# Inverse roots of norms and chains: from Sqrt on ScalarE to a power on GpSimd

## The chip, the cores and the metric

The kernel runs on one core of one Trainium2 chip. The metric is the device time of one execution in microseconds; three runs of the kernel before gave 1999.21, 1999.24 and 1999.36, median 1999.24. A profile of one further execution (1999.32 us) is what all readings below come from. Its own span, from the first to the last instruction, is 1997.5 us.

## The reference, cut to what matters

Four layers act on `x` of shape (8, 512, 32, 32), so on 8 images of 512 channels and 1024 pixels. The second works like this for each image, and inverse square roots appear in its group norm:

```python
# layer 0: attention without softmax, scaled by the largest singular value
f_x = relu(batchnorm(conv1x1(x, Wf, bf), gamma_f, beta_f))   # rsqrt(var + 1e-5)
g_x = relu(batchnorm(conv1x1(x, Wg, bg), gamma_g, beta_g))   # rsqrt(var + 1e-5)
h_x = conv1x1(x, Wh, bh)
z = einsum('bcn,bcm->bnm', f_x, g_x)
attn = z / svd(z)[0]
x = conv1x1(einsum('bnm,bcm->bcn', attn, h_x), Wv, bv) + x
# layer 1: group norm, then attention with softmax over 1024 pixels
h = group_norm(x)                                            # rsqrt(var + 1e-5)
q, k, v = wq @ h, wk @ h, wv @ h
x = x + wp @ (softmax(q.T k / sqrt(512)) applied to v)
# layer 2: a second attention, 128 channels, batch norm with given statistics
# layer 3: sign(x) times sign(W), batch norm with given statistics, a PReLU
```

## The kernel before, in words

All weights stay in SBUF, and the work runs in two parts.

The early part (to about 213 us) loads the eight images, computes the projections `f`, `g` and `h` of layer 0 and their batch statistics, and builds the combined weights of layer 1 (`wu`, `wo`). The norm of `f` and `g` needs one inverse root on 128 x 2 numbers (name `r0`). The singular value of `z` is found per pair of images by a chain of squarings of 128 x 128 matrices (`chain`, four of them): each step is two products on TensorE, an eviction of them from PSUM by VectorE or ScalarE, and a trace that is stored in a column of `tr`. A chain takes the root of its first trace near its start and needs it only at its end, where Ln and Exp on ScalarE turn the traces into the scale `rsig`. The first chain runs in the early part; the three others are slipped in between the matmuls of the images.

The main part goes through the eight images in the order 6, 7, 0, 1, 2, 3, 4, 5 (`fast`). For one image it runs these stages:

- `scores1`: the first attention's scores, with Strassen-like products of seven terms (`seven`), the exponentials on ScalarE (L347, L510, L511), one addition of two blocks on GpSimd (L341), and the row sums `esum` on VectorE (L515, L516). Between these, `enter` adds layer 0's result to the next image, takes its statistics and computes its group norm, with one inverse root on 128 x 4 numbers (name `r1`). The scale and bias that come out are used first when the next image is normalized (L440, L442), in the middle of `values1`.
- `make_v`: products of `h` and `wo`, again of seven terms. The first term of each is copied out of PSUM by ScalarE (L331) before TensorE may add the next to the same bank. After the first of the terms, `inverse_sums` adds the row sums over the partitions with a matmul (L775) and inverts them (L783).
- `values1` (L536), then the second attention (`project2` at L621 and L633, `scores2` at L754 with exponentials at L761, `values2` at L874), and `close2` and `leave` for the last layer.

The order on each engine is set by a scheduler that goes by its own estimates of durations, but for TensorE in the early chain, where the order of the program is kept. [...]

The inverse root is a helper, `rsqrt_eps`: VectorE writes `v = var + eps`, ScalarE takes `Sqrt` (L219), VectorE inverts it, and four more operations of VectorE make one Newton step. It is used for `r3` and `r2` (given statistics, at 12 us), for `r0`, and for `r1` once for each image. Beside the main path, a fallback with general softmax runs only when a check of the row sums fails; it isn't run here.

[...] `Sqrt`, `Ln` and `Exp` are in different loaded sets in this program, and the build puts a table load ahead of each change of set (the rows ACT_TABLE_LOAD).

## Time and profile before

| | |
|---|---|
| time, median of 3 | 1999.24 us |
| span of the profiled execution | 1997.5 us |
| mean granted clock of TensorE | 0.988 of full speed |
| ScalarE table loads | 29, of 1.283 us each |
| of these under `rsqrt_eps` (L219) | 9 |
| under the chains' root (L971) | 2 |
| Sqrt instructions | 11 in `rsqrt_eps`, 4 in chains, about 0.20 us each |
| idle times of TensorE over 0.06 us | 44, 44.1 us in all |

A row of a timeline reads: start in us, length in us, engine, line, operation, the tile written and the tiles read, shape, and how many instructions in a row were merged; in brackets the idle time before it and the work that ended it. fp32 matmuls stand in the trace as two records each. A row of busy times by stretch reads: the stretch, its length, then busy microseconds and number of instructions of TensorE, its weight loads, VectorE, ScalarE and GpSimd, then the granted clock of TensorE, the share of the DMA engines and GB/s.

### The profile page before, as it was taken

How to read it: one execution, taken by the hardware profiler on the slowest of the kernel's cores; microseconds unless marked ns; L12 is line 12 of the kernel's file. 1: busy time of each engine (PE TensorE's matmuls, PEld its weight loads, DVE VectorE, ACT ScalarE, POOL GpSimd, SP SyncE). 2: the span in 40 equal slices, each digit the busy share in tenths (PEclk: the TensorE clock that was granted, in tenths of full speed). 3: DMA queues.
4: the chain of work that ended last, by engine and by line, in shares of the span. 5: the costliest groups of instructions: out<-in, count | busy, mean ns of one | idle time of the engine just before them, and what ended most of it. 6: DMA issues, size and time to landing. Idle time of an engine off the chain costs nothing.

```text
span 1997.5 us, 16654 instructions
## 1 busy us (share of the span) xinstructions
PE 1936.9 (97%) x6262; PEld 997.3 (50%) x6262; DVE 1111.1 (56%) x1822; ACT 536.6 (27%) x838; POOL 187.9 (9%) x152
## 2 busy tenths in 40 slices
PE   8999899999999999999999999999999999999997
PEld 2377346544465445454465446444545446544653
DVE  3245577437863487536752576337653675256626
ACT  2132222134220342123311432034212431134114
POOL 0000000200011000200011000200020001101110
PEclk9989999999999999999999999999999999999999
DMA  9320000002000020001100020002000110010001
GB/s 330 127 74 1 6 6 11 1 11 85 6 11 0 11 84 17 0 0 32 68 11 1 22 77 13 0 11 85 11 0 1 42 53 11 0 32 21 11 1 54
DMA packets 26711, 66.99 MB, mean 34 GB/s; under 512 B 3760, under 2 KB 4016, under 8 KB 25984
## 3 DMA queue, kind: packets, MB, share of 16 engines
q1 hardware_dynamic: 25968, 65.09, 9.5%
q8 instruction: 51, 0.84, 0.2%
q0 software_dynamic: 224, 0.33, 0.1%
q10 hardware_dynamic: 432, 0.43, 0.1%
q14 instruction: 36, 0.29, 0.0%
HBM read 38.51 MB, written 18.87 MB: 29 GB/s over the span
## 4 chain that ended last, share of the span: by engine, by line
PE 92%; DVE 4%; ACT 3%; issue 1%; DMA 0%; DVEq 0%; ACTq 0%
PE bank L369 37%; PE bank L536 19%; PE bank L874 6%; PE bank L621 6%; PE bank L754 6%; PE bank L1122 4%; PE bank L633 3%; PE bank L650 3%; PE bank L392 2%; PE bank L670 1%; PE bank L925 1%; PE wide L1178 1%; PE bank L1232 1%; PE bank L926 1%; PE bank L775 1%; DVE e L326 1%
## 5 line engine op out<-in xcount | busy, mean ns | idle before, releaser
L536 PE MATMUL bank<-e,vt 128*128 128x512 f32 x768 | 334.0, 593 | 0.0
L536 PEld LDWEIGHTS bank<-e,vt 128*128 128x128 f32 x768 | 145.0, 190 | 175.4 <-issue 171.7
L369 PE MATMUL bank<-ut,h 128*128 128x512 f32 x384 | 183.3, 598 | 4.7 <-ACT e L331 4.7
L369 PE MATMUL bank<-us,hs 128*128 128x512 f32 x256 | 121.3, 596 | 0.5 <-DVE us L298 0.5
L326 DVE TENSOR_TENSOR e<-bank,e 128x512 f32<-128x512 f32 x128 | 87.7, 685 | 61.2 <-PE bank L369 59.9
L874 PE MATMUL bank<-e,tpg 128*128 128x512 f32 x256 | 114.6, 595 | 0.0
L754 PE MATMUL bank<-tpg 128*128 128x512 f32 x256 | 114.6, 592 | 0.0
L369 PEld LDWEIGHTS bank<-ut,h 128*128 128x128 f32 x384 | 70.6, 190 | 87.7 <-issue 73.5
L621 PE MATMUL bank<-xt,tpg 128*128 128x512 f32 x256 | 113.6, 592 | 0.0
L369 PE MATMUL bank<-wo,h 128*128 128x256 f32 x384 | 95.7, 389 | 18.3 <-ACT vt L331 18.3
L761 ACT ACTIVATE e<-bank 128x512 f32<-128x512 f32 x128 | 76.4, 597 | 88.3 <-PE bank L754 88.3
L369 PE MATMUL bank<-h,wu 128*128 128x512 f32 x192 | 92.1, 603 | 3.4 <-DVE h L442 3.4
L326 DVE TENSOR_TENSOR vt<-bank,vt 128x512 f32<-128x512 f32 x64 | 44.0, 687 | 90.2 <-PE bank L369 89.3
L341 POOL TENSOR_TENSOR ut<-ut 128x512 f32<-128x512 f32 x16 | 21.7, 1359 | 734.1 <-ACT ut L322 734.1
L766 DVE TENSOR_TENSOR esum<-esum,e 128x1024 f32<-128x1024 f32 x48 | 58.8, 1226 | 54.8 <-ACT e L761 54.8
L369 PEld LDWEIGHTS bank<-wo,h 128*128 128x128 f32 x384 | 72.4, 193 | 31.1 <-ACT vt L331 21.5
L341 POOL TENSOR_TENSOR e<-e 128x512 f32<-128x512 f32 x32 | 41.6, 1301 | 441.1 <-ACT e L320 388.3
L874 PEld LDWEIGHTS bank<-e,tpg 128*128 128x128 f32 x256 | 48.0, 190 | 63.9 <-issue 63.9
L754 PEld LDWEIGHTS bank<-tpg 128*128 128x128 f32 x256 | 48.6, 190 | 60.8 <-issue 58.6
L621 PEld LDWEIGHTS bank<-xt,tpg 128*128 128x128 f32 x256 | 47.9, 190 | 56.4 <-issue 55.0
L369 PEld LDWEIGHTS bank<-us,hs 128*128 128x128 f32 x256 | 47.3, 190 | 57.5 <-issue 51.4
L660 ACT ACTIVATE sg<-xt,rb 128x512 f16<-128x512 f32 x64 | 43.8, 717 | 103.6 <-DVE xt L652 100.9
(306 smaller groups left out, 2996.4 us busy)
## 6 DMA issues: line engine op xcount, KB each, us to landing
xt<-in_x SPq DMA_DIRECT2D x56, 512.0 KB
out<-both SPq DMA_DIRECT2D x64, 256.0 KB
rfull<-rsum SPq DMA_DIRECT2D x64, 128.0 KB
f_dram<-f SPq DMA_DIRECT2D x8, 256.0 KB
fb<-f_dram SPq DMA_DIRECT2D x8, 256.0 KB
w<-in_w SPq DMA_DIRECT2D x1, 1024.0 KB
q<-in_w_q SPq DMA_DIRECT2D x1, 1024.0 KB
k<-in_w_k SPq DMA_DIRECT2D x1, 1024.0 KB
```

The source lines that it names most:

```text
L326: nc.vector.tensor_tensor(dst, ps, u, ALU.add)
L341: nc.gpsimd.tensor_tensor(c22, c22, c12, ALU.add)
L369: mm(out=ps[:, q * w : (q + 1) * w], lhsT=lt(ka, kb, q, k), rhs=rhs(ka, kb, q, k), start=first and q == 0 and k == 0, stop=last and k == 1 ...
L536: mm(out=ps, lhsT=a[:, t, bass.ts(r_, P)], rhs=e[t], start=first and t == 0, stop=last and t == NTH - 1, skip_group_check=True,)
L621: mm(out=ps, lhsT=sbw["tpg"][:, cc, bass.ts(i, P)], rhs=xt[:, cc, half(h)], start=cc == 0, stop=cc == CC - 1,)
L633: mm(out=ps[:, i, :], lhsT=xt[:, cc, bass.ts(4 * h + i, P)], rhs=sbw["tpg"][:, cc, 2 * P : 3 * P], start=cc == 0, stop=cc == CC - 1,)
L650: mm(out=ps, lhsT=sbw["z"][:, bass.ts(oc, P)], rhs=att, start=True, stop=True)
L754: mm(out=ps, lhsT=pt[:, 0, bass.ts(t, P)], rhs=tt[:, 0, half(h)], start=True, stop=True,)
L761: nc.scalar.activation(e[:, half(h)], ps, AF.Exp, scale=float(P) ** -0.5)
L766: nc.vector.tensor_tensor(esum, esum, e, ALU.add)
L874: mm(out=banks[h], lhsT=gt[:, t, :], rhs=es[t][:, half(h)], start=t == 0, stop=t == NT - 1,)
L1122: mm(out=banks[i][side(h), :], lhsT=w0[i][:, cc, :], rhs=xt[:, cc, half(h)], start=cc == 0, stop=cc == CC - 1,)
```

## The change

The Sqrt on ScalarE and the reciprocal on VectorE after it are replaced, in both places, by one instruction of GpSimd that raises the number to the power -0.5. The exponent is a constant tile, set once by a memset. The Newton step of the norms stays as it was. The chain's Newton step for the root becomes one for the inverse root: four operations of VectorE where there were a reciprocal, three others and another reciprocal. Nothing else is edited; the scheduler places the instructions anew.

```diff
+    minus_half = const.tile([P, CC], F32, tag="minus_half", name="minus_half")
+    nc.gpsimd.memset(minus_half, -0.5)
...
         nc.vector.tensor_scalar(v, var, EPS, None, ALU.add)
-        nc.scalar.activation(e, v, AF.Sqrt)
-        nc.vector.reciprocal(r, e)
+        nc.gpsimd.tensor_tensor(r, v, minus_half[:, 0:n], ALU.pow)
         nc.vector.tensor_tensor(e, r, r, ALU.mult)
         nc.vector.tensor_tensor(e, e, v, ALU.mult)
         nc.vector.tensor_scalar(e, e, -0.5, 1.5, ALU.mult, ALU.add)
...
         root, half_ = column("root"), column("half_")
-        nc.scalar.activation(root, tr[:, 0:1], AF.Sqrt)
-        nc.vector.reciprocal(half_, root)
+        nc.gpsimd.tensor_tensor(root, tr[:, 0:1], minus_half[:, 0:1], ALU.pow)
+        nc.vector.tensor_tensor(half_, root, root, ALU.mult)
         nc.vector.tensor_tensor(half_, half_, tr[:, 0:1], ALU.mult)
-        nc.vector.tensor_tensor(root, root, half_, ALU.add)
-        nc.vector.tensor_scalar(root, root, 0.5, None, ALU.mult)
-        nc.vector.reciprocal(root, root)
+        nc.vector.tensor_scalar(half_, half_, -0.5, 1.5, ALU.mult, ALU.add)
+        nc.vector.tensor_tensor(root, root, half_, ALU.mult)
```

Line numbers in the text are those of the kernel before. In the kernel after, lines from about 202 on stand two further down as far as the helper, one further down from there to the chain's root, and the same after it.

## The prediction

> **What bounds the kernel now.** I read the page's busy times first, then the idle times ahead of TensorE, and then, for each idle time, the timelines of ScalarE and VectorE over the same microseconds.

> ```profile
> PE 1936.9 (97%) x6262; PEld 997.3 (50%) x6262; DVE 1111.1 (56%) x1822; ACT 536.6 (27%) x838; POOL 187.9 (9%) x152
> ...
> L219 ACT ACT_TABLE_LOAD x9 | 11.5, 1283 | 2.3 <-issue 2.2
> ```

> TensorE sets the time; ScalarE is busy 27%, so taking work off it is worth only what TensorE waits for it. The groups of ScalarE by shape show 29 table loads in all (9 at L219, 6 at L761, 4 at L998, 4 at L1001, 3 at L510, 2 at L971, 1 at L347), 37.2 us at 1283 ns. Where does TensorE wait behind one? Its timeline has 44 idle times, 44.1 us together. Seven lie at one place, the start of `make_v`, where the copy at L331 must empty a PSUM bank before TensorE may add to it. First ScalarE, then TensorE, of the second image:

> ```profile
> 536.94 1.06 ACT L511 ACTIVATE e<-e 128x1024 f32<-128x1024 f32 x1
> 538.02 1.28 ACT L219 ACT_TABLE_LOAD   x1
> 539.32 0.20 ACT L219 ACTIVATE r_e<-r_v 128x4 f32<-128x4 f32 x1
> 539.54 1.28 ACT L510 ACT_TABLE_LOAD   x1
> 540.84 0.63 ACT L510 ACTIVATE e<-e 128x512 f32<-128x512 f32 x1
> 541.37 0.57 ACT L331 COPY vt<-bank 128x512 f32<-128x512 f32 x1
> ```
> ```profile
> 536.42 1.89 PE L369 MATMUL bank<-wo,h 128*128 128x256 f32 x8
> 541.99 2.07 PE L369 MATMUL bank<-wo,h 128*128 128x256 f32 x4 [3.68 <-ACT vt L331]
> 544.03 1.74 PE L775 MATMUL bank<-esum,ones 128*64 128x512 f32 x4
> 545.71 1.99 PE L369 MATMUL bank<-so,hs 128*128 128x256 f32 x8
> 547.54 0.38 PE L925 MATMUL bank<-cur 128*128 128x128 f32 x2
> ```

> The Sqrt and the return to Exp stand between two exponentials, so the copy comes 2.8 us late. The next image's norm does not need its result for another 15 us or more. The last image has no next norm; it is the control:

> ```profile
> 1847.32 1.89 PE L369 MATMUL bank<-wo,h 128*128 128x256 f32 x8
> 1849.88 1.99 PE L369 MATMUL bank<-wo,h 128*128 128x256 f32 x8 [0.68 <-ACT vt L331]
> 1851.81 1.08 PE L775 MATMUL bank<-esum,ones 128*64 128x512 f32 x4
> 1852.81 1.99 PE L369 MATMUL bank<-so,hs 128*128 128x256 f32 x8
> 1854.64 1.67 PE L369 MATMUL bank<-wo,h 128*128 128x256 f32 x7
> ```

> The wait is 0.68 there, and the same 4 records of L775 take 1.0 instead of 1.7. So the idle time costs twice: the granted clock, by stretches, falls after it (the number ahead of the last two columns).

> ```profile
> 538.60:542.00 3.40, 0.01 (x1) 0.01 (x1) 2.46 (x11) 3.30 (x5) 0.00 (x0) 1.00 0.00 0
> 542.10:545.40 3.30, 3.30 (x8) 1.36 (x8) 3.14 (x4) 0.00 (x0) 0.00 (x0) 0.50 0.00 0
> ...
> 777.60:784.30 6.70, 6.04 (x14) 3.16 (x13) 5.82 (x4) 0.00 (x0) 0.00 (x0) 0.50 0.00 0
> 995.00:1000.00 5.00, 3.36 (x15) 1.69 (x14) 4.69 (x9) 2.29 (x4) 0.00 (x0) 1.00 0.00 0
> ```

> [...] L511 ends at 538.00, the load starts at 538.02, and the Sqrt starts 0.02 after the load. [...] 0.50 in stretches of 3.4 to 6.8 us after the three waits of 3.68, and 1.00 after the four of 1.64. [...]

> **The change part by part.**

> *Table loads.* In the order in which the changed kernel's instructions stand, ScalarE has 9 loads where it had 29: one at the start, and L998 and L1001 for each of four chains. Twenty are gone, 25.7 us of ScalarE. The six at L761 are worth nothing on the path: from the first matmul of L621 to the first of L874 it is 50.2 us in the third image, which has no such load (853.31 to 903.52), and 50.2 in the fourth, which has (1069.44 to 1119.65). L347 and L971 have no TensorE wait of L331's kind behind them. So what counts is `make_v`.

> I price it over the same 28 records: 16 of `wo,h` (in images one to seven 4 of them come later, 0.87 us), 4 of L775, 8 of `so,hs`. Last image: 1847.32 to 1854.64, 7.32. Second: 536.42 to 547.54 plus 0.87, 11.99. The first and third, read the same way, 298.47 to 310.75 and 771.21 to 784.30, give 13.15 and 13.96. The fourth to seventh give 8.38 (993.76 to 1001.27 plus 0.87). The excess over the control is 5.83, 4.67 and 6.64, sum 17.1, and 4 x 1.06 = 4.2.

> How much of it goes? In the first three images L510 would start at 538.00, the copy end near 539.15, and TensorE start then, 0.84 after it stopped. It then has all 8 records (1.73) and would reach L775 at 540.9. But L775 needs the row sums, and the new order on VectorE puts three L557 subtractions between them: from 537.4, small operations of 0.1, three of 0.62 and two sums of 1.2 give 542.1. A wait of 1.25 stays, with 0.15 above the control at the copy: 1.4 an image, 4.3 in three. Gain 17.1 - 4.3 = 12.8. It takes for granted that pieces of 0.84 and 1.25 no longer bring the half clock, as 1.64 and 1.81 (at 486.6) bring none. In the four others the sums end at 998.2 and TensorE reaches L775 at 998.14: all 4.2 goes. Together 17.0.

> *The power on Pool* (call p the time from VectorE's `r_v` to its reading of the result). The trace has none. From below: the nearest small Pool rows are 0.10 us (a memset of one column) and 0.31 (the 128x128 select), so p is at least about 0.3. [...] I take [...] p = 0.8[...].

> What p delays: in the new order VectorE reads the result one operation (0.62) after `r_v`, so past p = 0.5 VectorE stands still with the row sums queued behind it. At 0.8 that is 0.3 in each of three images, and 0.1 in each of four, where TensorE has as much slack: 1.3 in all. The first-layer norm (101 us) and the first image's norm (207 us) are on the path: Sqrt and reciprocal took 0.44 from the end of `r_v` (101.10 to 101.54), the power 0.8: 0.4 each, 0.8. In the first chain the power's reader is now ahead of the eviction at L945 (114.58); at p = 0.8 that ends near 115.7, and its product starts at 115.81: nothing. The other three roots land where VectorE has about 1 us idle (367) or more; even behind one Pool sum (1.27) they delay no matmul. [...]

> *The rest.* One VectorE operation fewer (0.15 to 0.18) per norm and root, hidden or in the 0.44; one memset of 0.1 at 5 us on an idle Pool. On Pool the power stands between the `e` sums and the `vt` sums, which start 15 us later (552.58 in the second image). No DMA is added; on SP one `fb` load moves one place.

> Sum: 17.0 - 1.3 - 0.8 = 14.9 of the span of 1997.5. The three timed runs are 1.7 to 1.9 us above that span, and I carry the difference over: 1999.24 - 14.9 = 1984.3, so 1984.

> **The rivals.**

> *Slower: the power is slow.* Place: VectorE's in-order queue after each `r_v`. Every microsecond of p costs about 10: three images, four images, two norms on the path and the first chain. The gain is 2.9 at p = 2.0 (12.8 - 4.5, 4.2 - 5.2, -3.2, -1.2), so it decides from p = 2.3. At p = 5 it is 1999.2 + 27 = 2026, and the half clock would return on top. For it: nothing in the trace bounds p closely. Against it: the Pool's simple rows run at 1.27 us for 512 columns, so its fixed cost is small.

> *A new wait keeps the clock low.* The wait for the row sums takes over, [...] the first three images keep the half clock. Then a stall of 4.85 (541.99 and 544.03 against 4 records' 0.87) shrinks to 2.4: 3 x 2.45 + 4.2 - 2.1 = 9.4, that is 1990. A middling p of 1.5 gives 7.9, or 1991, in the same region.

> *The loads were hidden anyway*, or waiting moves with them: 1999. Against it stands the control.

> **How the numbers follow.** Fast power with the clock kept, 0.60: 1984, by itself 1979 to 1988 (all 21.3 of excess gone at best; p to 1.1). New wait or middling p, 0.20: 1988 to 1995. Hidden or cancelling, 0.05: within 4 us of before. Slow power, 0.15. The measurement tells about 0.2%, 4 us, from no change. So faster 0.80, same 0.05, slower 0.15. The range takes in the first two cases and p to 2: 1979 to 1997, which leaves out the slow power and a little below.

> **What would show it.** Right: nine table loads; L331's wait in `make_v` 0.7 to 0.9; no half clock near 303, 542 and 777; Pool power rows under 1 us; L775 waiting about 1.2 for the row sums in images one to three. Wrong: power rows of 2 us and more, VectorE idle before the first Newton product, or half clock still in the first three images.

## The result and the profile after

| | before | after |
|---|---|---|
| time, median | 1999.30 us (1999.21 to 1999.52) | 1986.47 us (1985.89 to 1988.39) |
| ratio, 95% interval | | 0.9937 (0.992 to 0.9955) |
| span of the profiled execution | 1997.5 | 1984.6 |
| mean granted clock of TensorE | 0.988 | 0.992 |
| table loads of ScalarE | 29 | 9 |
| early part, to the first matmul of `make_v` | 298.47 | 298.86 |
| first three images, `make_v` start to `values1` start | 36.07, 34.69, 33.87 | 31.91, 31.69, 28.88 |
| fourth to seventh image, the same | 27.45 each | 27.01 each |
| last image, the same (the control) | 26.4 | 26.4 |

The change made the kernel 12.8 us faster. The stage rows are read off TensorE's timeline, as the start of the first `wo,h` matmul and of the first matmul of `values1`. They sum to 4.16 + 3.00 + 4.99 + 4 x 0.44 = 13.9 us gained in `make_v`. Of this 0.4 is lost in the early part, and 0.5 at the very end: behind the last VectorE instruction 5.43 us pass until the span ends, where before takes 4.89. No matmul is left there in either kernel; what makes this end longer was not looked into. All other stages agree within 0.02. That leaves the 13.0 by which the spans differ.

The page's busy times, and the table loads among ScalarE's groups by shape:

```profile
PE 1929.4 (97%) x6262; PEld 993.9 (50%) x6262; DVE 1104.4 (56%) x1807; ACT 507.8 (26%) x803; POOL 203.9 (10%) x168
```
```profile
L998 ACT ACT_TABLE_LOAD x4 | 5.1, 1283 | 0.1
L1001 ACT ACT_TABLE_LOAD x4 | 5.1, 1283 | 0.1
L1139 ACT ACT_TABLE_LOAD x1 | 1.3, 1283 | 2.1 <-issue 2.1
```

TensorE runs as many matmuls as before in 7.5 us less busy time, as the granted clock is higher (0.992 for 0.988); the rest of the gain is idle time. Here is `make_v` of the second image, ScalarE first and then TensorE:

```profile
533.17 1.06 ACT L512 ACTIVATE e<-e 128x1024 f32<-128x1024 f32 x1
534.13 0.62 ACT L511 ACTIVATE e<-e 128x512 f32<-128x512 f32 x1
534.65 0.58 ACT L332 COPY vt<-bank 128x512 f32<-128x512 f32 x1
```
```profile
532.64 1.89 PE L370 MATMUL bank<-wo,h 128*128 128x256 f32 x8
535.27 1.99 PE L370 MATMUL bank<-wo,h 128*128 128x256 f32 x8 [0.74 <-ACT vt L332]
538.72 1.08 PE L776 MATMUL bank<-esum,ones 128*64 128x512 f32 x4 [1.45 <-DVE esum L517]
539.73 1.99 PE L370 MATMUL bank<-so,hs 128*128 128x256 f32 x8
```

The two exponentials now stand back to back, and no load stands ahead of the copy. TensorE's wait for it fell from 3.68 to 0.74. The four records of the row-sum matmul take 1.08 instead of 1.74: TensorE stayed at full clock. In the stretches that answer to the half-clock ones of before, in the first three images, the granted clock (third number from the end) is 1.00:

```profile
301.50:308.30 6.80, 5.35 (x26) 3.77 (x26) 6.80 (x12) 0.58 (x1) 0.00 (x0) 1.00 0.00 0
535.20:542.00 6.80, 5.27 (x24) 3.70 (x25) 6.80 (x12) 0.61 (x2) 0.00 (x0) 1.00 0.00 0
767.00:773.80 6.80, 5.28 (x24) 3.71 (x25) 6.80 (x12) 0.60 (x2) 0.00 (x0) 1.00 0.00 0
```

But a second wait, of 1.45, is there for the row sums. VectorE's timeline of the same image shows where a part of it comes from:

```profile
532.86 0.15 DVE L220 TENSOR_SCALAR r_v<-bank 128x4 f32<-128x4 f32 x1
532.97 0.69 DVE L327 TENSOR_TENSOR e<-bank,e 128x512 f32<-128x512 f32 x1
534.14 0.16 DVE L222 TENSOR_TENSOR r_e<-r_r 128x4 f32<-128x4 f32 x1 [0.47 <-POOL r_r L221]
...
535.56 1.22 DVE L516 TENSOR_TENSOR esum<-esum,e 128x1024 f32<-128x1024 f32 x1
...
537.44 1.22 DVE L517 TENSOR_TENSOR esum<-esum,e 128x1024 f32<-128x1024 f32 x1
```

VectorE stands still for 0.47 us at the first Newton product, with both row sums queued behind it. GpSimd's timeline has the power of the second image and that of the fourth:

```profile
533.09 1.02 POOL L221 TENSOR_TENSOR r_r<-r_v,minus_half 128x4 f32<-128x4 f32 x1 [2.45 <-DVE r_v L220]
...
983.05 1.40 POOL L221 TENSOR_TENSOR r_r<-r_v,minus_half 128x4 f32<-128x4 f32 x1 [5.12 <-DVE r_v L220]
```

From the end of `r_v` to the reader it is 1.13 us in the first three images (533.01 to 534.14), and 1.51 in the fourth to seventh. There VectorE waits longer, and TensorE with it. First VectorE, then TensorE, in the fourth image:

```profile
982.82 0.15 DVE L220 TENSOR_SCALAR r_v<-bank 128x4 f32<-128x4 f32 x1
982.89 0.68 DVE L558 TENSOR_TENSOR scratch<-e 128x512 f32<-128x512 f32 x1
984.48 0.16 DVE L222 TENSOR_TENSOR r_e<-r_r 128x4 f32<-128x4 f32 x1 [0.91 <-POOL r_r L221]
```
```profile
984.64 1.99 PE L370 MATMUL bank<-wo,h 128*128 128x256 f32 x8 [0.67 <-ACT vt L332]
987.09 1.08 PE L776 MATMUL bank<-esum,ones 128*64 128x512 f32 x4 [0.46 <-DVE esum L517]
```

### The profile page after: what moved, and what is told of

Its sections match the earlier page's. It is cut to its first block, busy times and chain, and to the rows that moved or that the text cites. A ratio compares the mean times of both kernels' runs of the same rounds, so it can differ in the third digit from the quotient of the medians.

```text
span 1984.6 us, 16624 instructions
## 1 busy us (share of the span) xinstructions
PE 1929.4 (97%) x6262; PEld 993.9 (50%) x6262; DVE 1104.4 (56%) x1807; ACT 507.8 (26%) x803; POOL 203.9 (10%) x168
## 4 chain that ended last, share of the span: by engine, by line
PE 92%; DVE 5%; ACT 2%; POOL 1%; issue 1%; DMA 0%; DVEq 0%; ACTq 0%
PE bank L370 36%; PE bank L537 19%; PE bank L875 6%; PE bank L622 6%; PE bank L755 6%; PE bank L1122 4%; PE bank L634 3%; PE bank L651 3%; PE bank L393 2%; PE bank L671 1%; PE bank L926 1%; PE bank L1232 1%; PE wide L1178 1%; PE bank L927 1%; PE bank L776 1%; DVE e L327 1%
```

## The experiments

The theory: the gain is the Sqrt and its two table loads leaving the place ahead of the copy in the seven norms, with the half clock that the wait brought. What is left over against the control is the time that VectorE stands behind the power. The rivals: the gain comes from fewer loads in general, or from the chains; or only a load's place matters, and the power is no cause of any gain. Before was run again beside the experiments. Its median is 1999.02 us beside the unused Sqrt, the doubled power, the late Newton step and the second of the kernels with a moved Sqrt, and 1998.38 beside the other four.

### Which part of the change: the norms alone, the chains alone

Each kernel takes one hunk of the change and leaves the other as it was before.

```diff
norms only:
-        nc.gpsimd.tensor_tensor(root, tr[:, 0:1], minus_half[:, 0:1], ALU.pow)
+        nc.scalar.activation(root, tr[:, 0:1], AF.Sqrt)
...
chains only:
-        nc.gpsimd.tensor_tensor(r, v, minus_half[:, 0:n], ALU.pow)
+        nc.scalar.activation(e, v, AF.Sqrt)
+        nc.vector.reciprocal(r, e)
```

> The power for the norms alone; the chains keep Sqrt and the old Newton step. If the prediction is right that the chains' root loads stand where TensorE does not wait, this is the whole gain: 1986 to 1987.5. Rival (part of the gain is the chains'): 1989 or more.

> The power for the chains alone; the norms keep Sqrt. Same theory: nothing gained, 1998 to 2000.5. Rival: 1996 or less.

Norms alone: 1987.12 us, ratio 0.9946 (0.9929 to 0.9962). Chains alone: 1998.66, ratio 1.0001 (0.9993 to 1.001). So the gain is the norms', and the chains add nothing that can be measured, though their part removes seven loads: 16 are left with the norms alone, 9 with both. ScalarE's timeline with the norms alone shows why such a load is free:

```profile
361.18 1.28 ACT L972 ACT_TABLE_LOAD   x1
362.48 0.20 ACT L972 ACTIVATE root<-tr 128x1 f32<-128x1 f32 x1
368.50 0.37 ACT L940 COPY cur<-bank 128x256 f32<-128x256 f32 x1 [5.83 <-PE bank L927]
```

After the chain's root ScalarE has nothing to do for 5.83 us.

### The loads put back: an unused Sqrt beside the power

After, with a Sqrt of the same numbers on ScalarE whose result nobody reads. It is added work; nothing is left out.

```diff
+        idle = pool.tile([P, n], F32, tag=name + "_i", name=name + "_i")
+        nc.scalar.activation(idle, v, AF.Sqrt)
         nc.gpsimd.tensor_tensor(r, v, minus_half[:, 0:n], ALU.pow)
```

> The kernel after, plus one Sqrt on ScalarE of the same numbers into a tile that nobody reads, in the helper. The roots still come from the power. Theory (the table loads ahead of the copy are the whole cause, not the Sqrt's result being waited for, and not VectorE's reciprocal): waits of 3.7 and 1.6 return, the half clock returns in the first three images, time 1997 to 2002. Rival (the gain came from taking ScalarE out of the norm's chain): 1987 to 1989.

2005.57 us, ratio 1.0034 (1.0028 to 1.0041): the whole gain goes, and 6.5 us more. The waits of 3.68 and 1.64 for the copy are back, and so is the half clock of the first three images. Nobody waits for the Sqrt's result, so the loads ahead of the copy suffice as cause. The time is above what I had expected, and the trace shows one reason that the prediction had ruled out, in the sixth image. First TensorE there, then the stretch of that wait, the one after it, and the stretch of the same wait in the seventh image:

```profile
1431.12 1.13 PE L372 MATMUL bank<-wo,h 128*128 128x256 f32 x4 [1.64 <-ACT vt L334]
1432.60 1.73 PE L778 MATMUL bank<-esum,ones 128*64 128x512 f32 x4 [0.35 <-DVE esum L519]
```
```profile
1429.48:1432.89 3.41, 1.42 (x6) 0.88 (x8) 2.91 (x6) 1.57 (x3) 0.47 (x1) 1.00 0.00 0
1432.89:1436.31 3.42, 3.42 (x9) 1.70 (x6) 3.07 (x5) 0.00 (x0) 0.00 (x0) 0.50 0.02 5
1644.52:1647.93 3.41, 1.77 (x9) 1.24 (x8) 2.50 (x7) 2.59 (x4) 1.40 (x1) 1.00 0.00 0
```

A wait of 1.64, with one of 0.35 for the row sums behind it, was followed by half clock. The same two waits in the fourth, fifth and seventh image were not, and the traces show one thing that differs. In before, from 200 us on, the granted clock changes at 207.49, 214.32, 303.07, 309.89, 542.00, 545.41, 777.52, 784.35 and 1989.25, which are 2, 26, 2, 68, 1, 68, 2 and 353 steps of 3.413 us apart. In after it changes at 206.30, 213.13 and 1977.82, 2 and 517 steps apart. I lay a grid of such steps over this trace too, from the change at 1432.89. In the sixth image both waits fall into one cell of it (1429.48 to 1432.89), of which TensorE is busy for 1.42 us. In the seventh, an edge at 1647.93, 63 steps on, parts them, and the emptier cell has 1.77. The last section has the cells of before and after.

The power's own cost stays on top: the row sums are waited for 0.91 in the first two images and 0.35 in the fourth to seventh, where TensorE in before has no such wait. By stages, the 5.8 us between the profiled spans are 1.0 in the early part, 1.3 in the first three images together, 4 x 0.42 in the four later ones, 1.65 more in the sixth for its half clock, and 0.2 at the end. The time of this kernel varies from 2000.24 to 2007.84. Against the start of the span the grid lies 1.19 us earlier in after than in before (206.30 for 207.49). If it also moves from one execution to the next, the number of half-clock cells can differ. That this makes the spread is not shown, as unprofiled executions have no trace.

### The power's price: the power twice

After, with the power of every norm computed twice, one behind the other. This too only adds work.

```diff
+        nc.gpsimd.tensor_tensor(e, v, minus_half[:, 0:n], ALU.pow)
         nc.gpsimd.tensor_tensor(r, v, minus_half[:, 0:n], ALU.pow)
```

> The kernel after, with each norm's power computed twice in a row on GpSimd, the first into a tile that is overwritten. The power takes 1.02 us alone and 1.40 beside VectorE's subtraction, so the result comes 1.0 to 1.4 later. Theory of the prediction (about 10 us for each us of the power): 3 x 1.0 + 4 x 1.4 + 0.7 + 1.0 = 10.3 more, 1996.8, perhaps with half clock in the first three images on top. Rival (the power is mostly hidden): within 2 us of 1986.5.

2000.33 us, ratio 1.0008 (0.9999 to 1.0017): 13.9 above after for about 1.0 us in each norm. I had expected 10.3, with 1.4 in each of the four later images; the second power takes 1.00 there. GpSimd's timeline in the fourth image, and TensorE's in the second:

```profile
994.10 1.39 POOL L221 TENSOR_TENSOR r_e<-r_v,minus_half 128x4 f32<-128x4 f32 x1 [5.11 <-DVE r_v L220]
995.47 1.00 POOL L222 TENSOR_TENSOR r_r<-r_v,minus_half 128x4 f32<-128x4 f32 x1
```
```profile
541.04 1.99 PE L371 MATMUL bank<-wo,h 128*128 128x256 f32 x8 [0.74 <-ACT vt L333]
545.47 1.98 PE L777 MATMUL bank<-esum,ones 128*64 128x512 f32 x4 [2.43 <-DVE esum L518]
```

The wait for the copy is what it was in after. The wait for the row sums went from 1.45 to 2.43, and from 0.46 to 1.43 in the four later images: 3 x 0.98 + 4 x 0.97 = 6.8 us. So VectorE's queue behind the power is on the path in all seven images, microsecond for microsecond. The early part grew by 4.8: about 2.0 are the two norms there (the first image's wait went from 4.05 to 5.02), and a half-clock stretch at 207.6 that lasts 13.65 us instead of 6.83 holds most of the rest. Two more such stretches of 3.41 us, at 545.5 and 781.0, come with the longer waits; the second and third image's `make_v` grew by 1.64 and 1.68 more than the wait. Together this is 14.9, against 14.8 between the two profiled spans.

### The power kept, its reader moved: a late Newton step

After, with the Newton step, scale and bias issued where the normalization of the next image uses them, and no longer right behind the power. The instructions are the same.

```diff
-        nc.vector.tensor_tensor(e, r, r, ALU.mult)
-        nc.vector.tensor_tensor(e, e, v, ALU.mult)
-        nc.vector.tensor_scalar(e, e, -0.5, 1.5, ALU.mult, ALU.add)
-        nc.vector.tensor_tensor(r, r, e, ALU.mult)
-        return r
+        def rest():
+            nc.vector.tensor_tensor(e, r, r, ALU.mult)
...
+            return r
+        return rest if later else rest()
...
-        sc, bi = norm
+        sc, bi = norm.pop()()
```

> The kernel after, with the Newton step, scale and bias of the group norm given to the scheduler at the head of normal instead of in enter; the power stays where it was. Theory: behind the power VectorE stands still (0.47 us in the first three images, 0.91 in the next four) with the row sums queued behind the first Newton product, so TensorE waits for the row sums 1.45 and 0.46. With the product behind the sums that wait falls to about 0.65 in three images and to nothing in four: 3 x 0.8 + 4 x 0.46 = 4.2 us less, 1982.3. Rival (the row sums are late for another reason, the subtractions ahead of them): 1986 unchanged.

1982.08 us, ratio 0.9916 (0.9899 to 0.9932), 4.4 below after. VectorE, then TensorE, of the second image:

```profile
535.58 1.22 DVE L526 TENSOR_TENSOR esum<-esum,e 128x1024 f32<-128x1024 f32 x1
...
537.32 0.15 DVE L224 TENSOR_TENSOR r_e<-r_r 128x4 f32<-128x4 f32 x1
```
```profile
534.33 1.99 PE L374 MATMUL bank<-wo,h 128*128 128x256 f32 x8 [0.74 <-ACT vt L336]
536.85 1.08 PE L785 MATMUL bank<-esum,ones 128*64 128x512 f32 x4 [0.53 <-DVE esum L526]
```

The first Newton product now comes behind both row sums and has no idle time before it. TensorE's wait for the sums is 0.53 in the first three images and gone in the other four. From the waits: 3 x 0.92 + 4 x 0.46 = 4.6 us, against 4.4 measured. With that, `make_v` of the fourth to seventh image takes 26.48, where the control takes 26.4. In the first three images only half of the 0.92 is the power's wait. From the end of `r_v` to the end of the second row sum it is 5.65 us in after and 4.74 here; 0.47 of the difference is the time that VectorE stood still, and 0.44 are five small operations of the norm that also left the place ahead of the sums. In the four later images nearly all is the wait (0.91 of 0.96).

### Sqrt kept, only its place moved

Two kernels start from before and keep Sqrt and reciprocal, for the norms and the chains. In the first they are part of the late step, as above. In the second their input also depends on the inverted row sums (which are multiplied by zero and added), so that the scheduler can't place the Sqrt before `make_v`'s copy.

```diff
+        def rest(gate=None):
+            if gate is not None:          # second kernel only
+                nc.vector.scalar_tensor_tensor(v, gate, 0.0, v, ALU.mult, ALU.add)
+            nc.scalar.activation(e, v, AF.Sqrt)
+            nc.vector.reciprocal(r, e)
...
-                hb = split_h(env, normal(env, nxt))
+                hb = split_h(env, normal(env, nxt, gate=r[:, 0, 0:CC]))
```

> The kernel before with Sqrt, reciprocal and the rest of the norm given at the head of normal, but without a dependence. The scheduler then puts Sqrt behind the second of the two exponentials, so one load stands ahead of the copy where two stood in the first three images, and the return to Exp moves to scores2. Theory (each load ahead of the copy counts, and row sums no longer come after loads): wait 2.3 in the first three images, 1.64 in the next four, excess 3 x 1.7 + 4 x 1.1 over sqrt_gated's 1978.9: 1988, plus up to 3 for each half-clock window that comes. Rival (the first three images' loss needs both loads to bring the half clock or nothing changes): 1995 or more.

> The kernel before, still with Sqrt on ScalarE, but the group norm's Sqrt is made to depend on the inverted row sums (its input gets zero times them added), so that it can only run after the first copies of make_v. Theory (not the Sqrt but the place of its table loads costs): the seven waits fall to 0.7 and the half clock goes, though 27 table loads remain; the extra loads lie in values1 and scores2, where TensorE does not wait. 1982, as good as newton_late or better. Rival (table loads cost wherever they stand, or ScalarE has to lose the work): 1995 to 1999.

The first: 1989.66 us, ratio 0.9959 (0.9945 to 0.9974). The scheduler moved the Sqrt only behind both exponentials, so that one load instead of two stands ahead of the copy. ScalarE, then TensorE, of the second image:

```profile
535.54 1.28 ACT L221 ACT_TABLE_LOAD   x1
536.83 0.21 ACT L221 ACTIVATE r_e<-r_v 128x4 f32<-128x4 f32 x1
536.95 0.57 ACT L335 COPY vt<-bank 128x512 f32<-128x512 f32 x1
```
```profile
537.57 2.54 PE L373 MATMUL bank<-wo,h 128*128 128x256 f32 x6 [2.25 <-ACT vt L335]
```

A wait of 2.25 stays in the first three images and one of 1.64 in the other four. The half clock came in the first two images (3.41 us each) and not in the third. On the grid of 3.413 us from the change at 538.00, the second image's wait lies in one cell, of which TensorE is busy for 1.16 us. An edge at 770.11, 68 steps on, cuts the third's in two, and those cells have 2.03 and 2.55:

```profile
534.59:538.00 3.41, 1.16 (x6) 0.70 (x5) 3.41 (x5) 2.89 (x5) 0.00 (x0) 1.00 0.00 0
766.70:770.11 3.41, 2.03 (x11) 1.47 (x9) 3.41 (x6) 3.00 (x4) 0.00 (x0) 1.00 0.01 2
770.11:773.53 3.42, 2.55 (x11) 1.30 (x11) 3.15 (x6) 0.81 (x3) 0.00 (x0) 1.00 0.00 0
```

The second: 1978.85 us, ratio 0.99 (0.9884 to 0.9917), with 26 table loads in its trace. ScalarE and TensorE again:

```profile
531.40 0.62 ACT L521 ACTIVATE e<-e 128x512 f32<-128x512 f32 x1
531.92 0.58 ACT L337 COPY vt<-bank 128x512 f32<-128x512 f32 x1
...
543.56 1.28 ACT L223 ACT_TABLE_LOAD   x1
544.85 0.20 ACT L223 ACTIVATE r_e<-r_v 128x4 f32<-128x4 f32 x1
```
```profile
532.55 1.99 PE L375 MATMUL bank<-wo,h 128*128 128x256 f32 x8 [0.74 <-ACT vt L337]
535.07 1.08 PE L786 MATMUL bank<-esum,ones 128*64 128x512 f32 x4 [0.53 <-DVE esum L527]
```

The Sqrt and its load stand 12 us later, in a part of ScalarE's queue where nobody waits, and TensorE's waits are those of the late Newton step. This version beats both kernels, by 20.2 us and by 7.6. Sqrt on ScalarE was not the fault; the place of its loads was.

### Power and Sqrt mixed

The late Newton step, with Sqrt for the batch norms and the first image's norm, where the result is wanted at once, and the power for the seven other norms and the chains.

```diff
-        nc.gpsimd.tensor_tensor(r, v, minus_half[:, 0:n], ALU.pow)
+        if power:                      # from the second image's norm on
+            nc.gpsimd.tensor_tensor(r, v, minus_half[:, 0:n], ALU.pow)
+        else:
+            nc.scalar.activation(e, v, AF.Sqrt)
+            nc.vector.reciprocal(r, e)
```

> Sqrt on ScalarE for the two norms whose root TensorE waits for (the first layer's and the first image's), the power with the late Newton step for the seven others and the chains. Theory (loads off the path cost nothing, and the power costs only where it is waited for): the waits of newton_late without its 1.8 us in the early part, equal to sqrt_gated: 1979 to 1980.5. Rival (the loads that sqrt_gated keeps cost something after all): 1977 or less.

1979.07 us, ratio 0.9906 (0.9889 to 0.9922), with 11 loads. Its range (1978.80 to 1979.46) and that of the gated Sqrt with 26 loads (1978.78 to 1979.35) cover each other. Fifteen loads, 19.2 us of ScalarE, cost nothing that can be measured where nobody waits. In both kernels the early part is 1.4 us shorter than in before (297.0). In their traces the half-clock stretch near 136 us lasts 13.65 us, and in before's and after's 17.07. At the 0.50 granted there, I estimate that the 3.41 us less are worth at most 1.7, enough for it. Whether the other executions have it too isn't known.

## Why the prediction was right, and where its sum was off

The sign, the region and the mechanism held: 1984.0 was said and 1986.47 measured, 2.1 us less gain than the 14.9 of the sum. That it came so near is in part luck. Against the sum, by the two profiles, the first three images gave 0.25 more and the early part 0.4 more, the four later images 2.0 less, and the end of the kernel, which the sum left out, 0.5 less. By its steps:

- *Table loads in the first three images.* Right. The prediction left 12.8 less 0.9 for the power, 11.9, and the stages gained 4.16 + 3.00 + 4.99 = 12.15. The copy's wait is 0.74, where 0.84 was worked out, and the row-sum wait 1.45 where 1.25 + 0.3 was. Two errors met there. VectorE's stall is 0.47 and not 0.3, but without it 0.98 of the wait would be left and not 1.25, since the sums come 0.1 earlier after the stage's start than the addition of durations had it, and TensorE 0.15 later.
- *The loads at L761 and in the chains are worth nothing.* Right: the stages are unchanged, the chains alone give 1.0001, and the mixed kernel equals one with 15 more loads.
- *The four later images.* Here the sum failed. "All 4.2 goes", less 0.4 for the power, was 3.8; 4 x 0.44 = 1.76 came. The step that failed is p = 0.8, my assumption, which no trace had shown: from `r_v` to its reader it is 1.51 there. VectorE stands 0.91 and TensorE 0.46, where 0.1 was put down. The late Newton step took just this wait away and left 26.48 against the control's 26.4. These 2.0 us are as much as the whole miss, since the other errors nearly cancel. In the first three images the time from `r_v` to its reader was too small as well, 1.13 for 0.8, and the row sums made up for it.
- *The power elsewhere.* 0.8 was charged to the two early norms. From the end of `r_v` to the first Newton product they lost 0.34 and 0.64, and the early part as a whole lost 0.4. The two powers at 12 us are like the later ones: the first of the program starts at 11.60, right behind the VectorE operation that releases it (its end is 11.59), and the two take 1.04 and 1.00, where the later ones of 128x4 take 1.02 or 1.40.
- *The half clock.* The outcome was right, 1.00 in all three places. The ground given for it, that waits of 1.64 bring none, was wrong as a rule: the idle Sqrt showed half clock behind 1.64 and 0.35. There TensorE was busy for 1.42 of 3.41 us (42%, from 1429.48 to 1432.89), and the granted clock of the next 3.42 us was 0.50. In after there was room: 1.99 us of matmuls lie between the waits of 0.74 and 1.45, so no cell of the grid can hold more idle time than the 1.45, and the emptiest cells of the three stages are busy for 1.96, 2.08 and 2.24 us.
- *The rivals.* "Hidden" falls by the norms alone. "A new wait keeps the clock low" is half there: the new wait came, and the clock stayed up. "Slow power" had its turning point at p = 2.3 by a slope of 10. The doubled power, at p of about 2.1 and 2.5, gave 2000.33 against 1999.02: the slope held (6.8 in seven images and about 2 in two early norms), and the half clock came on top, as that rival said. The slope's term for the chains was not tested, as only the norms' power was doubled.
- *The signs.* Nine loads, the copy's wait of 0.74 and the full clock came as listed. The row-sum wait was 1.45 for about 1.2. Not all powers stayed under 1 us: those of 128x4 take 1.02 and 1.40. VectorE idle before the first Newton product stood among the signs of being wrong, and it came (0.47 and 0.91). The sum itself had 0.3 of it, so the sign was set too tight.
- *The best case of the range.* "All 21.3 of excess gone" would be 1978; the two last kernels reach 1978.85 and 1979.07 by taking away both the loads at the copy and the wait behind the power.

## What to carry to other kernels

Before replacing a function because its table loads are many, ask of each load which instruction stands behind it in ScalarE's queue and who waits for that; here 15 loads were free and seven places cost all. Where a small step is slow, move its consumer (4.4 us with the late Newton step): put the first reader of the result behind the work in its queue that the critical engine waits for. An image or pass that lacks the suspected work is a good control, and the excess of the others over it bounds what can be gained there.

## What the runs showed of the hardware

- *The power on GpSimd* takes 0.55 us for 128x1, 0.70 for 128x2 and 1.02 for 128x4 where nothing disturbs it. From these rows I estimate about 0.39 and 0.16 for each column.
- *Beside some VectorE instructions it takes longer.* In after, it does so in three kinds of place, always where it starts inside a VectorE instruction that reads both its inputs from SBUF: the 128x4 of the fourth to seventh image, and the 128x1 of the third and the fourth chain. The rows of these two chains, GpSimd and VectorE:

```profile
360.66 0.98 POOL L972 TENSOR_TENSOR root<-tr,minus_half 128x1 f32<-128x1 f32 x1 [12.06 <-DVE tr L961]
360.54 0.69 DVE L602 TENSOR_TENSOR o_b<-o_b,o_a 128x512 f32<-128x512 f32 x1
567.61 1.47 POOL L972 TENSOR_TENSOR root<-tr,minus_half 128x1 f32<-128x1 f32 x1 [7.14 <-DVE tr L961]
567.45 1.22 DVE L309 TENSOR_TENSOR hs<-h 128x1024 f32<-128x1024 f32 x1
```
